# Turning node features with VectorE's 32x32 transposes and a hop through DRAM, in a two-layer graph network

## The chip, the cores and the metric

The kernel runs on one core of one Trainium2 chip. The metric is device time in microseconds (us), the median of the runs. The core's engines work side by side, each on its own in-order stream of instructions: TensorE (PE in the profile; its weight loads are PEld), VectorE (DVE), ScalarE (ACT), GpSimd (POOL) and the queue engine SyncE (SP), which here only issues DMA transfers. They wait for one another through semaphores.

## What is computed

There are 16 independent batches of 1024 nodes with 128 features each. Layer 0 is an attention with a gate, layer 1 has four heads with a tanh in place of a softmax, and each layer ends with a residual sum and a layer norm. Cut to what matters:

```python
# B, N, D, H = 16, 1024, 128, 4
def layer0(x, adj):
    h = x @ Ww.T + Wb
    e = (h @ A) @ h.T
    e = e + e.T
    scores = where(adj > 0, e, 0.0)
    attention = softmax(scores, axis=1) * adj
    hp = relu(attention @ h)
    ic = sigmoid(hp @ wi_u + x @ wi_x)         # fc, oc alike
    return oc * tanh(ic * hp + fc * x)

def layer1(X, adj):
    h = X @ conv_w[head] + conv_b[head]        # for each of 4 heads
    scores = h @ attn_w[head] @ h.T
    hh = relu(tanh(adj * scores) @ h)
    return relu(relu(mean_over_heads(hh)) + X)

x = layernorm(x + layer0(x, adj))
x = layernorm(x + layer1(x, adj))
```

Everything is float32. A layer norm needs the nodes on the partitions (a row of features along the free dimension), while the products of layer 1 need the features on the partitions. So each batch has two turns of a 1024 x 128 matrix: the result x1 of the first layer norm becomes x1T, and the sum over the heads, which stands as features x nodes, becomes rows again before the last layer norm.

## The kernel before

`P` and `D` are 128, `NB` is 8 (blocks of 128 nodes), `NH` is 2 (halves of 512 columns), `BH` is 4. Numbers as L385 in the profile are lines of the whole kernel. The pools, and the late weights, which are issued behind batch 0's loads on the sync queue:

```python
    consts = ctx.enter_context(tc.tile_pool(name="consts", bufs=1))
    adjp = ctx.enter_context(tc.tile_pool(name="adjp", bufs=2 * NB + 1))
    sb = ctx.enter_context(tc.tile_pool(name="sb", bufs=2))
    ps_sc = ctx.enter_context(tc.tile_pool(name="ps_sc", bufs=4, space=PSUM))
    ps_acc = ctx.enter_context(tc.tile_pool(name="ps_acc", bufs=1, space=PSUM))
# ...
    def load_late_weights():
        nc.sync.dma_start(cw_in[0:1], conv_b.rearrange("(o h) d -> o h d", o=1))
        nc.sync.dma_start(cw_in[1:P], conv_w[:, 0 : D - 1, :].rearrange("h f d -> f h d"))
        nc.sync.dma_start(cw_last, conv_w[:, D - 1 : D, :].rearrange("h f d -> f h d"))
        nc.sync.dma_start(aw, attn_w.rearrange("h i j -> i h j"))
```

Layer 0 is a generator: each `yield` is a point at which the caller goes on with something else. Its scores, softmax and products (some lines cut):

```python
    def layer0(b):
        xTb = sb.tile([P, N], F32, tag="xT", name=f"xT_{b}")
        nc.sync.dma_start(xTb, xT[b])
        adj_t[b] = []
        for j in range(NB):
            t = adjp.tile([P, N], F32, tag="adj", name=f"adj_{b}_{j}")
            nc.sync.dma_start(t, adjT[b, ts(j, P), :])
            adj_t[b].append(t)
        xb = sb.tile([P, NB, D], F32, tag="x", name=f"x_{b}", bufs=1)
        nc.sync.dma_start(xb, x[b].rearrange("(k p) d -> p k d", p=P))
        if b == 0:
            load_late_weights()
    # ... project_T -> qT, yield; project rows -> h, yield
        def score(j):
            raw[j] = sb.tile([P, N - j * P], F32, tag=f"raw{j}", name=f"raw_{b}_{j}", bufs=1)
            scored[j] = []
            for q in range(NH):
                # ... blocks known by symmetry are turned from raw (L261); a product gives
                # the others (L266), which ScalarE evicts to raw (L269)

        def front(j):
            s = sb.tile([P, N], F32, tag="s0", name=f"s0_{b}_{j}", bufs=3)
            for at0, at1, e in scored.pop(j):
                if at0 < at1:
                    nc.vector.scalar_tensor_tensor(
                        s[:, at0:at1], adj_t[b][j][:, at0:at1], 0.0, e,
                        op0=ALU.is_gt, op1=ALU.mult,
                    )
            nmax = sb.tile([P, 1], F32, tag="nmax", name=f"nmax_{b}_{j}", bufs=4)
            nc.vector.tensor_reduce(nmax, s, AX.X, ALU.max, negate=True)
            z = sb.tile([P, 1], F32, tag="z", name=f"z_{b}_{j}", bufs=4)
            nc.scalar.activation(s, s, AF.Exp, bias=nmax, accum_out=z)
            if b:
                nc.gpsimd.tensor_mul(s, s, adj_t[b][j])
            held[j] = s, z

        def middle(j):
            s, z = held[j]
            if not b:
                nc.vector.tensor_mul(s, s, adj_t[b][j])
            rz = sb.tile([P, 1], F32, tag="rz", name=f"rz_{b}_{j}", bufs=4)
            nc.vector.reciprocal(rz, z)
            hz = sb.tile([P, D], F32, tag="hz", name=f"hz_{b}_{j}", bufs=4)
            nc.scalar.mul(hz, h[:, j, :D], rz)
            held[j] = s, hz

        def back(j):
            s, hz = held.pop(j)
            for q in range(NH):
                nc.tensor.matmul(
                    acc[:, ts(q, 512)], hz, s[:, ts(q, 512)],
                    start=(j == 0), stop=(j == NB - 1),
                )

        ahead = 0 if b else 1
        for j in range(ahead + 1):
            score(j)
        front(0)
        yield
        for j in range(NB):
            if j + 1 < NB:
                if j + 1 + ahead < NB:
                    score(j + 1 + ahead)
                front(j + 1)
                yield
            middle(j)
            if j:
                back(j - 1)
            yield
        back(NB - 1)
    # ... hp rows, gate, tanh (L331 to L370)
        x1 = sb.tile([P, NB, D + 1], F32, tag="x1", name=f"x1_{b}")
        nc.gpsimd.memset(x1[:, :, 0:1], 1.0)
        yield from layernorm(u, x1[:, :, 1 : D + 1], f"0_{b}")
        x1_t[b] = x1
```

`BETWEEN` drives it: layer 0 of batch b + 1 advances one `yield` after each of the first 24 of the 32 steps of layer 1 of batch b. The turn of x1, one step of layer 1 and the end of layer 1:

```python
    def turn_x1(b):
        x1T = sb.tile([P, N], F32, tag="x1T", name=f"x1T_{b}")
        for q in range(NH):
            pt = small(f"pt1_{b}_{q}")
            for i in range(BH):
                nc.tensor.transpose(pt[:, ts(i, P)], x1_t[b][:, q * BH + i, 0:D], ident)
            nc.scalar.copy(x1T[:, ts(q, 512)], pt)
        x1T_t[b] = x1T

    def layer1_step(b, hd, m):
        x1T, h1, uT = x1T_t[b], h1_t[b, m], u_t[b, hd]
        adj = adj_t[b][m]
        # ... acc: the PSUM tile of this head
        s = sb.tile([P, N], F32, tag="s1", name=f"s1_{b}_{hd}_{m}", bufs=4)
        for q in range(NH):
            ps = ps_sc.tile([P, 512], F32, tag="sc", name=f"sc1_{b}_{hd}_{m}_{q}")
            nc.tensor.matmul(ps, x1T[:, ts(m, P)], uT[:, ts(q, 512)], start=True, stop=True)
            nc.vector.tensor_mul(s[:, ts(q, 512)], ps, adj[:, ts(q, 512)])
        nc.scalar.activation(s, s, AF.Tanh)
        def back():
            for q in range(NH):
                nc.tensor.matmul(
                    acc[:, ts(q, 512)], h1[:, ts(hd, D)], s[:, ts(q, 512)],
                    start=(m == 0), stop=(m == NB - 1),
                )
            # at m == NB - 1: the relu of acc is added to sum_t[b] (L431, L433)
        push(back)

    def layer1_end(b):
        x1 = x1_t[b][:, :, 1 : D + 1]
        y = sb.tile([P, NB, D], F32, tag="u", name=f"y_{b}", bufs=1)
        for q in range(NH):
            pt = small(f"pt2_{b}_{q}")
            for i in range(BH):
                nc.tensor.transpose(pt[:, ts(i, P)], sum_t[b][:, ts(q * BH + i, P)], ident)
            rows = slice(q * BH, (q + 1) * BH)
            nc.vector.scalar_tensor_tensor(
                y[:, rows, :], pt.rearrange("p (k d) -> p k d", d=D), 1.0 / H, x1[:, rows, :],
                op0=ALU.mult, op1=ALU.add,
            )
        nc.vector.scalar_tensor_tensor(y, y, 0.0, x1, op0=ALU.max, op1=ALU.add)
        yield
        yield from layernorm(y, y, f"1_{b}")
        nc.gpsimd.dma_start(out[b].rearrange("(k p) d -> p k d", p=P), y)
```

The order of everything:

```python
    first, join = layer0(0), None
    for step, _ in enumerate(first):
        if step == 2 * NB:
            join = join_weights()
        if step >= 2 * NB:
            next(join, None)
    for _ in join:
        pass
    turn_x1(0)

    BETWEEN = range(24)
    ENDING = (DELAY, DELAY + 2, DELAY + 4)
    end = None
    for b in range(B):
        nxt = layer0(b + 1) if b + 1 < B else None
        for hd in range(H):
            for m in range(NB):
                layer1_step(b, hd, m)
                if end is not None and hd == 0 and m in ENDING:
                    next(end, None)
                if nxt is not None and hd * NB + m in BETWEEN:
                    next(nxt, None)
                last = hd == H - 1
                # ... see the diff
        end = layer1_end(b)
    while pending:
        pending.popleft()()
    for _ in end:
        pass
```

`push` holds a step's second product back for `DELAY` = 2 steps, so that ScalarE has its tanh ready.

Of the kernel before, what the change touches and what calls it, by code (L numbers as in the profile page):

```python
# [21 lines left out]
def two_layer_adjacency_kernel(  # L22
# [28 lines left out]
    adjp = ctx.enter_context(tc.tile_pool(name="adjp", bufs=2 * NB + 1))  # L51
    sb = ctx.enter_context(tc.tile_pool(name="sb", bufs=2))
    ps_sc = ctx.enter_context(tc.tile_pool(name="ps_sc", bufs=4, space=PSUM))
    ps_acc = ctx.enter_context(tc.tile_pool(name="ps_acc", bufs=1, space=PSUM))
# [10 lines left out]

    a_in = consts.tile([P, P], F32, name="a_in")
    nc.sync.dma_start(a_in, A)
    ww_in = consts.tile([P, P], F32, name="ww_in")
    nc.sync.dma_start(ww_in, Ww)
# [12 lines left out]
    nc.gpsimd.memset(wb_row[:, D:G], 0.0)  # L82
    gate_u, gate_x = ident_g[:, D : D + 3], wwT_g[:, D : D + 3]

    for t, ws in ((gate_x, (wi_x, wf_x, wo_x)), (gate_u, (wi_u, wf_u, wo_u))):
        for g, w in enumerate(ws):
            nc.scalar.dma_start(t[:, g : g + 1], w.rearrange("(d o) -> d o", o=1))
        if t is gate_x:
            nc.scalar.dma_start(wb_row[:, :D], Wb.partition_broadcast(P))

    def load_late_weights():
        nc.sync.dma_start(cw_in[0:1], conv_b.rearrange("(o h) d -> o h d", o=1))
        nc.sync.dma_start(cw_in[1:P], conv_w[:, 0 : D - 1, :].rearrange("h f d -> f h d"))
        nc.sync.dma_start(cw_last, conv_w[:, D - 1 : D, :].rearrange("h f d -> f h d"))
        nc.sync.dma_start(aw, attn_w.rearrange("h i j -> i h j"))
# [118 lines left out]

    adj_t, x_t, x1_t = {}, {}, {}


    def layer0(b):
# [28 lines left out]
        held, raw, scored = {}, {}, {}  # L247

        def score(j):

            raw[j] = sb.tile([P, N - j * P], F32, tag=f"raw{j}", name=f"raw_{b}_{j}", bufs=1)
            scored[j] = []
            for q in range(NH):
                ps = ps_sc.tile([P, 512], F32, tag="sc", name=f"sc0_{b}_{j}_{q}")
                turned = min(max(j - q * BH, 0), BH)
                for i in range(turned):
                    k = q * BH + i  # L260
                    nc.tensor.transpose(ps[:, ts(i, P)], raw[k][:, ts(j - k, P)], ident)  # L261
                lo, at = q * 512 + turned * P, (q + 1) * 512
                scored[j].append((q * 512, lo, ps[:, : turned * P]))
                if lo < at:
                    new = raw[j][:, lo - j * P : at - j * P]
                    nc.tensor.matmul(  # L266
                        ps[:, turned * P :], qT[:, ts(j, P)], xTb[:, lo:at], start=True, stop=True
                    )
                    nc.scalar.activation(  # L269
                        new, ps[:, turned * P :], AF.Identity, bias=h[:, j, G - 1 : G]  # L270
                    )
                    scored[j].append((lo, at, new))

        def front(j):

            s = sb.tile([P, N], F32, tag="s0", name=f"s0_{b}_{j}", bufs=3)
            for at0, at1, e in scored.pop(j):
                if at0 < at1:
                    nc.vector.scalar_tensor_tensor(  # L279
                        s[:, at0:at1], adj_t[b][j][:, at0:at1], 0.0, e,  # L280
                        op0=ALU.is_gt, op1=ALU.mult,
                    )
            nmax = sb.tile([P, 1], F32, tag="nmax", name=f"nmax_{b}_{j}", bufs=4)
            nc.vector.tensor_reduce(nmax, s, AX.X, ALU.max, negate=True)  # L284
            z = sb.tile([P, 1], F32, tag="z", name=f"z_{b}_{j}", bufs=4)
            nc.scalar.activation(s, s, AF.Exp, bias=nmax, accum_out=z)  # L286
            if b:
                nc.gpsimd.tensor_mul(s, s, adj_t[b][j])  # L288
            held[j] = s, z

        def middle(j):

            s, z = held[j]
            if not b:
                nc.vector.tensor_mul(s, s, adj_t[b][j])
# [84 lines left out]
    def turn_x1(b):  # L380
        x1T = sb.tile([P, N], F32, tag="x1T", name=f"x1T_{b}")
# [89 lines left out]
    ENDING = (DELAY, DELAY + 2, DELAY + 4)  # L471
    end = None
    for b in range(B):
        nxt = layer0(b + 1) if b + 1 < B else None
        for hd in range(H):
            for m in range(NB):
# [8 lines left out]
                if last:  # L485
                    if m == NB - 4:
# [8 lines left out]
                elif m == NB - 3:  # L495
# [45 lines left out]
```

## Time and profile before

| what | value |
|---|---|
| time, median of 3 runs | 2555.05 us (2553.41 to 2555.42) |
| span of the profiled execution | 2551.7 us |
| GpSimd busy | 384.0 us, 15% of the span |
| DMA | 94.29 MB, mean 37 GB/s |
| products `sc` and `acc` of layer 1 on TensorE (L415, L421) | 963.9 and 962.0 us busy |
| products that turn x1 (L385) | 128, busy 17.7 us in sum |
| products that turn the head sums (L443) | 128, busy 16.8 us in sum |
| additions that take the turned sums from PSUM (L446) | 32 of 128x512, 686 ns each |
| copies of x1T out of PSUM on ScalarE (L386) | 32 of 128x512, 588 ns each |

How to read it: busy time is given for each engine and for each group of instructions, as a sum and as the mean of one. A group's line names the engine, the operation, the tile written, the tiles read and the shape. Idle time stands with what ended it. TensorE's instructions overlap one another, so the distance from one start to the next tells more of what it can do than the length of one. Every float32 product is listed as two instructions, a float32 transpose as one. DMA times run from the issue to the landing.

### The profile page before, as it was taken

The numbers are of one execution on the slowest core, as the hardware profiler recorded it, in microseconds if no ns is written. First come the engines' busy times: TensorE is split into PE (matmuls) and PEld (weight loads), VectorE is DVE, ScalarE is ACT, GpSimd is POOL, SyncE is SP. The second block draws the span as 40 slices with busy tenths as digits, with TensorE's granted clock in tenths as the row PEclk, the third lists the DMA queues.
The fourth block names the chain that finished last, engine by engine and source line by source line (L and its number), as shares of the span: only waits on it lengthen the run. The fifth ranks groups of instructions, "written<-read, shape, count | busy, mean of one in ns | idle before, by whom it ended". The sixth has DMA issues, their size and how long they took to land.

```text
span 2551.7 us, 20009 instructions
## 1 busy us (share of the span) xinstructions
PE 2504.9 (98%) x6818; PEld 1183.2 (46%) x6818; DVE 1423.7 (56%) x2977; ACT 1084.5 (43%) x1541; POOL 384.0 (15%) x211
## 2 busy tenths in 40 slices
PE   6999999999999999999999999999999999999997
PEld 3444444444444444444444444444444444444443
DVE  6555646555475554755456565564655646555454
ACT  4444444444443444444444344443444444444432
POOL 0110202102021110211202011020210202112000
PEclk9999999999999999999999999999999999999999
DMA  5002020020200102011020110202002020010000
GB/s 181 12 1 83 8 83 9 4 79 8 83 9 25 58 9 83 9 42 50 1 83 9 50 42 1 83 9 74 17 1 83 9 83 9 16 51 9 1 9 9
DMA packets 42269, 94.29 MB, mean 37 GB/s; under 512 B 3894, under 2 KB 21686, under 8 KB 42167
## 3 DMA queue, kind: packets, MB, share of 16 engines
q1 hardware_dynamic: 38855, 84.55, 10.5%
q0 software_dynamic: 2304, 8.39, 1.1%
q8 instruction: 54, 0.88, 0.2%
q14 instruction: 48, 0.39, 0.1%
q10 hardware_dynamic: 1008, 0.07, 0.0%
HBM read 84.61 MB, written 8.39 MB: 36 GB/s over the span
## 4 chain that ended last, share of the span: by engine, by line
PE 87%; DVE 7%; ACT 2%; issue 1%; SPq 1%; DMA 1%; POOL 0%; ACTq 0%; POOLq 0%
PE sc L415 32%; PE acc L421 32%; PE acc L305 8%; PE pR L394 4%; PE pT_u L197 3%; PE sc L266 2%; DVE s L279 2%; PE sc L261 2%; DVE nmax L284 1%; DVE s L416 1%; ACT s L417 1%; PE pt L340 1%; PE pR_h L239 1%; PE pT_q L197 1%; DVE st L180 1%
## 5 line engine op out<-in xcount | busy, mean ns | idle before, releaser
L416 DVE TENSOR_TENSOR s<-sc,adj 128x512 f32<-128x512 f32 x1024 | 683.4, 686 | 787.3 <-PE sc L415 772.3
L415 PE MATMUL sc<-uT,x1T 128*128 128x512 f32 x2048 | 963.9, 593 | 8.1 <-DVE s L279 8.1
L421 PE MATMUL acc<-s,h 128*128 128x512 f32 x2048 | 962.0, 592 | 0.0
L417 ACT ACTIVATE s<-s 128x1024 f32<-128x1024 f32 x512 | 541.5, 1058 | 834.1 <-DVE s L416 830.8
L421 PEld LDWEIGHTS acc<-s,h 128*128 128x128 f32 x2048 | 387.6, 190 | 491.3 <-issue 490.5
L415 PEld LDWEIGHTS sc<-uT,x1T 128*128 128x128 f32 x2048 | 382.1, 190 | 463.3 <-issue 391.5
L288 POOL TENSOR_TENSOR s<-s,adj 128x1024 f32<-128x1024 f32 x120 | 283.1, 2359 | 1494.8 <-PE sc L266 782.7
L286 ACT ACTIVATE s<-s,nmax 128x1024 f32<-128x1024 f32 x128 | 147.0, 1149 | 274.2 <-DVE nmax L284 272.1
L305 PE MATMUL acc<-s,hz 128*128 128x512 f32 x512 | 241.3, 593 | 5.9 <-ACT hz L299 5.9
L279 DVE SCALAR_TENSOR_TENSOR s<-adj,sc 128x512 f32<-128x512 f32 (+3 forms) x160 | 83.9, 526 | 157.5 <-ACT raw L269 89.2
L284 DVE TENSOR_REDUCE nmax<-s 128x1 f32<-128x1024 f32 x128 | 156.2, 1220 | 4.4
L305 PEld LDWEIGHTS acc<-s,hz 128*128 128x128 f32 x512 | 96.6, 190 | 129.0 <-issue 118.6
L269 ACT ACTIVATE raw<-sc,h 128x512 f32<-128x512 f32 (+1 forms) x192 | 107.2, 575 | 91.9 <-PE sc L266 90.4
L266 PE MATMUL sc<-xT,qT 128*128 128x512 f32 (+3 forms) x384 | 145.1, 487 | 0.0
L197 PE MATMUL pT_u<-x1T,ms 128*128 128x512 f32 x256 | 123.2, 604 | 0.1
L279 DVE SCALAR_TENSOR_TENSOR s<-adj,raw 128x512 f32<-128x512 f32 (+1 forms) x192 | 111.0, 598 | 7.3 <-ACT raw L269 4.7
L394 PE MATMUL pR<-cw,x1T 128*128 128x512 f32 x256 | 114.9, 592 | 0.0
L185 POOL TENSOR_TENSOR rs<-rs,mhalf 128x8 f32<-128x8 f32 x32 | 52.8, 1651 | 288.8 <-DVE rs L184 166.9
L397 ACT COPY h<-pR 128x512 f32<-128x512 f32 x128 | 74.9, 585 | 48.8 <-PE pR L394 48.8
L433 DVE SCALAR_TENSOR_TENSOR sum<-acc,sum 128x512 f32<-128x512 f32 x96 | 61.9, 686 | 46.4 <-PE acc L421 46.4
L352 POOL TENSOR_TENSOR u<-x,gate 128x1024 f32<-128x1024 f32 x16 | 30.5, 1907 | 342.5 <-DVE gate L350 342.5
L299 ACT ACTIVATE hz<-h,rz 128x128 f32<-128x128 f32 x128 | 50.4, 394 | 74.5 <-DVE rz L297 74.5
(89 smaller groups left out, 1126.7 us busy)
## 6 DMA issues: line engine op xcount, KB each, us to landing
adj<-in_adjT_dram SPq DMA_DIRECT2D x128, 512.0 KB, 3.7
xT<-in_xT_dram SPq DMA_DIRECT2D x16, 512.0 KB, 5.8
x<-in_x_dram SPq DMA_DIRECT2D x16, 512.0 KB, 5.1
out_dram<-y POOLq DMA_DIRECT2D x16, 512.0 KB, 3.9
aw<-in_L_gnn_attn_w_dram SPq DMA_DIRECT2D x1, 256.0 KB, 4.3
cw_in<-in_L_gnn_conv_w_dram SPq DMA_DIRECT2D x1, 254.0 KB
a_in<-in_L_gnn_A_dram SPq DMA_DIRECT2D x1, 64.0 KB, 2.3
ww_in<-in_L_gnn_Ww_dram SPq DMA_DIRECT2D x1, 64.0 KB, 2.4
```

The source lines that it names most:

```text
L197: nc.tensor.matmul(ps, w, src[:, ts(q, 512)], start=True, stop=True)
L266: nc.tensor.matmul(ps[:, turned * P :], qT[:, ts(j, P)], xTb[:, lo:at], start=True, stop=True)
L279: nc.vector.scalar_tensor_tensor(s[:, at0:at1], adj_t[b][j][:, at0:at1], 0.0, e, op0=ALU.is_gt, op1=ALU.mult,)
L284: nc.vector.tensor_reduce(nmax, s, AX.X, ALU.max, negate=True)
L286: nc.scalar.activation(s, s, AF.Exp, bias=nmax, accum_out=z)
L288: nc.gpsimd.tensor_mul(s, s, adj_t[b][j])
L305: nc.tensor.matmul(acc[:, ts(q, 512)], hz, s[:, ts(q, 512)], start=(j == 0), stop=(j == NB - 1),)
L394: nc.tensor.matmul(ps, x1T_t[b][:, ts(k, P)], cw.rearrange("p h d -> p (h d)"), start=True, stop=True)
L415: nc.tensor.matmul(ps, x1T[:, ts(m, P)], uT[:, ts(q, 512)], start=True, stop=True)
L416: nc.vector.tensor_mul(s[:, ts(q, 512)], ps, adj[:, ts(q, 512)])
L417: nc.scalar.activation(s, s, AF.Tanh)
L421: nc.tensor.matmul(acc[:, ts(q, 512)], h1[:, ts(hd, D)], s[:, ts(q, 512)], start=(m == 0), stop=(m == NB - 1),)
```

## The change

The kernel after turns x1 (batches 1 to 15) and the head sums (batches 0 to 14) without TensorE. VectorE transposes each 32x32 block of the tile in place of the whole, the result is written to a scratch tensor in DRAM, and four reads bring the blocks back to where a whole transpose would have put them. It is meant to take work from TensorE and copies from ScalarE, at the price of a way through DRAM that lasts longer; so the turn of x1 moves from step 4 of the last head to step 0, and the end of layer 1 waits three steps between its turn and its addition. Batch 0's x1 and batch 15's sums, beside which nothing else could run, keep the identity products.

Together with this goes another schedule for batch 0, whose layer 0 has nothing to run beside. The scores are no longer computed one block ahead, the multiplication by the adjacency goes to GpSimd as in the other batches, the late weights are loaded on GpSimd's queue rather than behind the loads of batch 0, x is loaded behind the first adjacency tile, and the joining of the layer 1 weights starts at step 5 instead of at step 16. The adjacency pool has one tile less. The projection for the next head comes at step 4 instead of step 5.

The diff, without blank lines and with one cut:

```diff
--- before.py
+++ after.py
@@ -48,9 +48,10 @@
     BH = NB // NH
     consts = ctx.enter_context(tc.tile_pool(name="consts", bufs=1))
-    adjp = ctx.enter_context(tc.tile_pool(name="adjp", bufs=2 * NB + 1))
+    adjp = ctx.enter_context(tc.tile_pool(name="adjp", bufs=2 * NB))
     sb = ctx.enter_context(tc.tile_pool(name="sb", bufs=2))
     ps_sc = ctx.enter_context(tc.tile_pool(name="ps_sc", bufs=4, space=PSUM))
+    dram = ctx.enter_context(tc.tile_pool(name="dram", bufs=2, space=bass.MemoryType.DRAM))
     ps_acc = ctx.enter_context(tc.tile_pool(name="ps_acc", bufs=1, space=PSUM))
     ctx.enter_context(tc.manual_schedule())
@@ loads of Ww and A change places; wb_row goes from the scalar to the sync queue: cut @@
 def load_late_weights():
-        nc.sync.dma_start(cw_in[0:1], conv_b.rearrange("(o h) d -> o h d", o=1))
-        nc.sync.dma_start(cw_in[1:P], conv_w[:, 0 : D - 1, :].rearrange("h f d -> f h d"))
-        nc.sync.dma_start(cw_last, conv_w[:, D - 1 : D, :].rearrange("h f d -> f h d"))
-        nc.sync.dma_start(aw, attn_w.rearrange("h i j -> i h j"))
+        nc.gpsimd.dma_start(cw_in[0:1], conv_b.rearrange("(o h) d -> o h d", o=1))
+        nc.gpsimd.dma_start(cw_in[1:P], conv_w[:, 0 : D - 1, :].rearrange("h f d -> f h d"))
+        nc.gpsimd.dma_start(cw_last, conv_w[:, D - 1 : D, :].rearrange("h f d -> f h d"))
+        nc.gpsimd.dma_start(aw, attn_w.rearrange("h i j -> i h j"))
@@ -212,6 +212,21 @@
                 bias_row.unsqueeze(1).to_broadcast([P, BH, D]),
             )
+    Q = 32
+    def turn(dst, src, name):
+        t = sb.tile([P, N], F32, tag="turn", name=f"turn_{name}", bufs=1)
+        nc.vector.transpose(t.rearrange("p (k d) -> p k d", d=P), src)
+        d = dram.tile([P, N], F32, tag="turn", name=f"dram_{name}")
+        nc.sync.dma_start(d, t)
+        dv = d.rearrange("(a i) (k c j) -> c i k a j", i=Q, c=P // Q, j=Q)
+        for c in range(P // Q):
+            nc.sync.dma_start(
+                dst[ts(c, Q)].rearrange("i (k a j) -> i k a j", a=P // Q, j=Q), dv[c]
+            )
     adj_t, x_t, x1_t = {}, {}, {}
@@ -224,10 +239,11 @@
             t = adjp.tile([P, N], F32, tag="adj", name=f"adj_{b}_{j}")
             nc.sync.dma_start(t, adjT[b, ts(j, P), :])
             adj_t[b].append(t)
-        xb = sb.tile([P, NB, D], F32, tag="x", name=f"x_{b}", bufs=1)
-        nc.sync.dma_start(xb, x[b].rearrange("(k p) d -> p k d", p=P))
-        if b == 0:
-            load_late_weights()
+            if j == 0:
+                xb = sb.tile([P, NB, D], F32, tag="x", name=f"x_{b}", bufs=1)
+                nc.sync.dma_start(xb, x[b].rearrange("(k p) d -> p k d", p=P))
+                if b == 0:
+                    load_late_weights()
         qT = sb.tile([P, N], F32, tag="qT0", name=f"qT0_{b}", bufs=1)
         h = sb.tile([P, NB, G], F32, tag="h0", name=f"h0_{b}", bufs=1)
@@ -244,15 +260,15 @@
         yield
         acc = ps_acc.tile([P, N], F32, tag="acc0", name=f"acc0_{b}")
-        held, raw, scored = {}, {}, {}
-        def score(j):
+        held, raw = {}, {}
+        def front(j):
             raw[j] = sb.tile([P, N - j * P], F32, tag=f"raw{j}", name=f"raw_{b}_{j}", bufs=1)
-            scored[j] = []
+            s = sb.tile([P, N], F32, tag="s0", name=f"s0_{b}_{j}", bufs=3)
             for q in range(NH):
                 ps = ps_sc.tile([P, 512], F32, tag="sc", name=f"sc0_{b}_{j}_{q}")
                 turned = min(max(j - q * BH, 0), BH)
@@ -260,7 +276,7 @@
                     k = q * BH + i
                     nc.tensor.transpose(ps[:, ts(i, P)], raw[k][:, ts(j - k, P)], ident)
                 lo, at = q * 512 + turned * P, (q + 1) * 512
-                scored[j].append((q * 512, lo, ps[:, : turned * P]))
+                parts = [(q * 512, lo, ps[:, : turned * P])]
                 if lo < at:
                     new = raw[j][:, lo - j * P : at - j * P]
                     nc.tensor.matmul(
@@ -269,30 +285,23 @@
                     nc.scalar.activation(
                         new, ps[:, turned * P :], AF.Identity, bias=h[:, j, G - 1 : G]
                     )
-                    scored[j].append((lo, at, new))
-        def front(j):
-            s = sb.tile([P, N], F32, tag="s0", name=f"s0_{b}_{j}", bufs=3)
-            for at0, at1, e in scored.pop(j):
-                if at0 < at1:
-                    nc.vector.scalar_tensor_tensor(
-                        s[:, at0:at1], adj_t[b][j][:, at0:at1], 0.0, e,
-                        op0=ALU.is_gt, op1=ALU.mult,
-                    )
+                    parts.append((lo, at, new))
+                for at0, at1, e in parts:
+                    if at0 < at1:
+                        nc.vector.scalar_tensor_tensor(
+                            s[:, at0:at1], adj_t[b][j][:, at0:at1], 0.0, e,
+                            op0=ALU.is_gt, op1=ALU.mult,
+                        )
             nmax = sb.tile([P, 1], F32, tag="nmax", name=f"nmax_{b}_{j}", bufs=4)
             nc.vector.tensor_reduce(nmax, s, AX.X, ALU.max, negate=True)
             z = sb.tile([P, 1], F32, tag="z", name=f"z_{b}_{j}", bufs=4)
             nc.scalar.activation(s, s, AF.Exp, bias=nmax, accum_out=z)
-            if b:
-                nc.gpsimd.tensor_mul(s, s, adj_t[b][j])
+            nc.gpsimd.tensor_mul(s, s, adj_t[b][j])
             held[j] = s, z
         def middle(j):
             s, z = held[j]
-            if not b:
-                nc.vector.tensor_mul(s, s, adj_t[b][j])
             rz = sb.tile([P, 1], F32, tag="rz", name=f"rz_{b}_{j}", bufs=4)
             nc.vector.reciprocal(rz, z)
             hz = sb.tile([P, D], F32, tag="hz", name=f"hz_{b}_{j}", bufs=4)
@@ -309,15 +318,10 @@
-        ahead = 0 if b else 1
-        for j in range(ahead + 1):
-            score(j)
         front(0)
         yield
         for j in range(NB):
             if j + 1 < NB:
-                if j + 1 + ahead < NB:
-                    score(j + 1 + ahead)
                 front(j + 1)
                 yield
             middle(j)
@@ -378,6 +382,10 @@
     x1T_t, h1_t, u_t = {}, {}, {}
     def turn_x1(b):
+        if b:
+            x1T_t[b] = sb.tile([P, N], F32, tag="x1T", name=f"x1T_{b}")
+            turn(x1T_t[b], x1_t[b][:, :, 0:D], f"x1_{b}")
+            return
         x1T = sb.tile([P, N], F32, tag="x1T", name=f"x1T_{b}")
         for q in range(NH):
             pt = small(f"pt1_{b}_{q}")
@@ -437,7 +445,11 @@
     def layer1_end(b):
         x1 = x1_t[b][:, :, 1 : D + 1]
         y = sb.tile([P, NB, D], F32, tag="u", name=f"y_{b}", bufs=1)
-        for q in range(NH):
+        if b + 1 < B:
+            turn(y.rearrange("p k d -> p (k d)"), sum_t[b].rearrange("p (k d) -> p k d", d=P), f"sum_{b}")
+            yield
+            nc.vector.scalar_tensor_tensor(y, y, 1.0 / H, x1, op0=ALU.mult, op1=ALU.add)
+        for q in range(NH if b + 1 == B else 0):
             pt = small(f"pt2_{b}_{q}")
             for i in range(BH):
                 nc.tensor.transpose(pt[:, ts(i, P)], sum_t[b][:, ts(q * BH + i, P)], ident)
@@ -455,9 +467,9 @@
     first, join = layer0(0), None
     for step, _ in enumerate(first):
-        if step == 2 * NB:
+        if step == 3:
             join = join_weights()
-        if step >= 2 * NB:
+        elif step > 3 and step % 2:
             next(join, None)
     for _ in join:
         pass
@@ -468,7 +480,7 @@
     BETWEEN = range(24)
-    ENDING = (DELAY, DELAY + 2, DELAY + 4)
+    ENDING = (DELAY, DELAY + 3, DELAY + 4, DELAY + 5)
     end = None
     for b in range(B):
         nxt = layer0(b + 1) if b + 1 < B else None
@@ -483,7 +495,7 @@
                 if last and b + 1 == B:
                     continue
                 if last:
-                    if m == NB - 4:
+                    if m == 0:
                         assert b + 1 in x1_t
                         turn_x1(b + 1)
                     elif m == NB - 3:
@@ -492,7 +504,7 @@
                         rows(b + 1, range(NB // 2))
                     elif m == NB - 1:
                         rows(b + 1, range(NB // 2, NB))
-                elif m == NB - 3:
+                elif m == NB - 4:
                     head_uT(b, hd + 1)
         end = layer1_end(b)
     while pending:
```

More of the change, by code (lines that the diff above doesn't have):

```diff
@@ L64, in two_layer_adjacency_kernel @@
     nc.gpsimd.memset(mhalf, -0.5)
+    ww_in = consts.tile([P, P], F32, name="ww_in")
+    nc.sync.dma_start(ww_in, Ww)
     a_in = consts.tile([P, P], F32, name="a_in")
     nc.sync.dma_start(a_in, A)
-    ww_in = consts.tile([P, P], F32, name="ww_in")
-    nc.sync.dma_start(ww_in, Ww)
     wb_col = consts.tile([P, 1], F32, name="wb_col")
@@ L82, in two_layer_adjacency_kernel @@
     nc.gpsimd.memset(wb_row[:, D:G], 0.0)
+    nc.sync.dma_start(wb_row[:, :D], Wb.partition_broadcast(P))
     gate_u, gate_x = ident_g[:, D : D + 3], wwT_g[:, D : D + 3]
@@ L87, in two_layer_adjacency_kernel @@
             nc.scalar.dma_start(t[:, g : g + 1], w.rearrange("(d o) -> d o", o=1))
-        if t is gate_x:
-            nc.scalar.dma_start(wb_row[:, :D], Wb.partition_broadcast(P))
     def load_late_weights():
-        nc.sync.dma_start(cw_in[0:1], conv_b.rearrange("(o h) d -> o h d", o=1))
-        nc.sync.dma_start(cw_in[1:P], conv_w[:, 0 : D - 1, :].rearrange("h f d -> f h d"))
-        nc.sync.dma_start(cw_last, conv_w[:, D - 1 : D, :].rearrange("h f d -> f h d"))
-        nc.sync.dma_start(aw, attn_w.rearrange("h i j -> i h j"))
+        nc.gpsimd.dma_start(cw_in[0:1], conv_b.rearrange("(o h) d -> o h d", o=1))
+        nc.gpsimd.dma_start(cw_in[1:P], conv_w[:, 0 : D - 1, :].rearrange("h f d -> f h d"))
+        nc.gpsimd.dma_start(cw_last, conv_w[:, D - 1 : D, :].rearrange("h f d -> f h d"))
+        nc.gpsimd.dma_start(aw, attn_w.rearrange("h i j -> i h j"))
     cw_in = sb.tile([P, H, D], F32, tag="s1", name="cw_in", bufs=4)
```

## The prediction, made before the change was run

> **What bounds the kernel now.** I read three things in turn: the page's busy shares, the list of what TensorE (PE) waited for, and the timelines of single engines around one batch boundary. The first line of the page's part 1 is busy time, share of the span, and instructions of each engine:
>
> ```profile
> PE 2504.9 (98%) x6818; PEld 1183.2 (46%) x6818; DVE 1423.7 (56%) x2977; ACT 1084.5 (43%) x1541; POOL 384.0 (15%) x211
> ```
>
> PE is idle for 46.8 us of 2551.7. Who made it wait (total us, times, longest):
>
> ```profile
> PE pt L385 <- DVE x L188: 12.4, 1, 12.4
> PE sc L415 <- DVE s L279: 8.1, 14, 0.6
> PE acc L305 <- ACT hz L299: 5.9, 7, 1.7
> ```
>
> The first and third are batch 0, whose layer 0 has nothing to overlap with; only the second belongs to the steady state, 0.58 us per batch. Most of the rest lies at the two ends of the run. So from batch 1 on PE has no holes, and every microsecond of PE work that disappears is a microsecond off the end, as long as no other engine makes PE wait. What the identity products cost PE is read from its timeline (start us, length us), at the turn of x1 and at the turn of the head sums:
>
> ```profile
> 207.41 1.04 PE L385 MATMUL pt<-ident,x 128*128 128x128 f32 x8
> 208.28 1.88 PE L415 MATMUL sc<-uT,x1T 128*128 128x512 f32 x4
> ...
> 240.99 1.04 PE L443 MATMUL pt<-ident,sum 128*128 128x128 f32 x8
> 241.86 1.88 PE L266 MATMUL sc<-xT,qT 128*128 128x512 f32 x4
> ```
>
> Start to start, eight products occupy PE for 0.87 us, 109 ns each, not the 273 ns that one is listed with.
>
> **What the skill says.** (1) The Trainium skill, "TensorE: Matmul & The Clock Gate", Part 4: PE-mode transpose, gives about 275 ns for a 128x128 transpose in a kernel. The trace has 273 ns as a duration, but these overlap; what can be saved is the 109 ns spacing. (2) "VectorE: DVE Perf Modes", The three transpose paths: VectorE transposes 32x32 blocks only, and the page warns that a DMA which transposes by strides is slow. The trace has no VectorE transpose; the change keeps 32 floats together, so its DMA moves runs of 128 bytes. (3) "DMA: Bandwidth & Descriptors", Anatomy of one DMA, puts some 2 us of fixed cost on each transfer. The trace agrees: the smallest loads, 0.5 KB, land after 2.4 us. (4) Same page, Why a DMA increments its semaphore by 16 and not by 1: a transfer uses the largest number of engines up to 16 that divides the slowest dimension on both sides, so 127 partitions get one engine. The trace agrees: after the load of 127 rows of conv weights the sync queue (SP) is stuck on its next issue for 14.19 us. The new reads have 32 partitions and so should use all 16.
>
> **The change, part by part.**
>
> *PE.* x1 is turned off PE for batches 1 to 15 and the sums for batches 0 to 14: 30 groups of eight, 30 x 0.87 = **26.1 us** less. All of it is on the bounding engine.
>
> *VectorE.* Each turn adds one 128x1024 transpose. I take 1.22 us, what the other one-pass 128x1024 operations here take (max-reduce 1.22, the add-relu 1.23): 30 x 1.22 = 36.6 us. The sums' two additions from PSUM (2 x 0.687) become one of about 1.22 us. VectorE goes from 1424 to about 1458 us, 58% of the span: not a bound. ScalarE loses 30 copies of 0.587 us, 17.6 us, which were beside other work. The end of layer 1 is now spread over steps 2, 5, 6 and 7 of the next batch's head 0 instead of 2, 4 and 6. I walked through the score buffers in PSUM: the 0.58 us wait comes while the row statistics (2.6 us) stand ahead of the masking. In the new order the score buffers come free in time, so I credit about half of it, **-4 us**.
>
> *The hop.* From the end of the transpose: one write to DRAM, a wait for it, four reads. The page's DMA part gives whole-tile transfers, and the DMA view of the first 12 us the small loads (packets, MB, share of 16 engines):
>
> ```profile
> out_dram<-y POOLq DMA_DIRECT2D x16, 512.0 KB, 3.9
> x<-in_x_dram SPq DMA_DIRECT2D x16, 512.0 KB, 5.1
> ```
> ```profile
> q10 hardware_dynamic: 1008, 0.07, 5.7%
> ```
>
> 5.7% of 16 x 12 us is 10.9 us for 1008 packets, about 11 ns each; nearly all of them carry 4 bytes. The one-engine weight load moved 508 runs of 512 bytes in about 14.2 us, 28 ns each. I interpolate 128 bytes at some 15 ns. A turn reads 4096 such runs, 256 per engine: 3.8 us. Write 3.9, semaphore 0.1, four issues at about 0.45 us each with the last starting 1.4 us after the first, then 2.4 us for a small transfer and the 64 runs of the last read (1 us): about **9 us**. Were a short run to cost as much as a 512-byte one, the reads take 7.2 us and the turn about 13.5.
>
> How long may it take? For x1, the timeline of VectorE at head 3, step 0:
>
> ```profile
> 192.14 2.14 DVE L188 TENSOR_SCALAR x<-u,mv,rs 128x128 f32<-128x128 f32 x8 [0.57 <-POOL rs L185]
> 194.20 2.48 DVE L416 TENSOR_TENSOR s<-sc,adj 128x512 f32<-128x512 f32 x4
> ```
>
> Normalization ends at 194.2, the masking of step 0 takes half of the next line, so the transpose runs from 195.5 to 196.7. The projection that reads x1T stays at step 5, where PE arrives at 211.72 - 0.87 = 210.85. Budget **14.2 us**, against 9. For the sums the transpose ends near 241.4 (masking of step 2 ends 240.2) and the addition comes behind the masking of step 5, which ended at 257.7 and would end near 255 without the 2.6 us of statistics. Budget about 13.7 us, and PE feels it only when VectorE is some 4 us late, for PSUM holds two steps. Both should be hidden. In the last batch there is no layer 0 beside it, so three steps are 3 x 3.44 = 10.3 us: a wait of perhaps **+1.5 us**, once.
>
> *Loads.* The adjacency pool shrinks from 17 to 16 tiles, so a load waits one step more. Layer 0 reads the tiles in batch order over 16 steps, starting two steps into head 0, and the loads take 3.7 us; this costs nothing. The hop stands in the same in-order SP queue, but the loads of the next batch cannot start before head 3 frees their buffers.
>
> *Batch 0.* Here the change undoes a schedule: no score is computed ahead, and the 128x1024 mask multiply goes from VectorE to GpSimd (1.22 against 2.36 us). Before, VectorE bounds this stage, 3.7 us per row block:
>
> ```profile
> 37.40 1.22 DVE L284 TENSOR_REDUCE nmax<-s 128x1 f32<-128x1024 f32 x1
> 38.54 1.22 DVE L295 TENSOR_TENSOR s<-s,adj 128x1024 f32<-128x1024 f32 x1
> ```
>
> After, the loop is a chain VectorE-ScalarE-VectorE: exp 1.2, row scaling 0.31, eviction of the new scores, their masking, max 1.22. With the listed durations row blocks 2 to 7 come every 4.6 down to 3.4 us, and three weight copies of 0.58 us are dropped into it. I get the last mask multiply on GpSimd ending at 49.7 and the last product there ending at 51.6 us, instead of 48.2. The joining of weights has left the tail, -1 us. Late weights on GpSimd's queue no longer block SP, but nobody waited for what was blocked. Net **+2.5 us**.
>
> Sum: 2555.05 - 26.1 - 4 + 1.5 + 2.5 = 2529; 3 us on top for small waits that I did not find: **2532 us**, 0.9% less.
>
> **Rivals.** *A. The turn arrives late for PE.* Four reads of short runs might cost over 30 ns a run, or the read may wait longer for the write to DRAM. For it: the budgets are only 5 us above my estimate, and no 128-byte transfer is in the trace. Against: the 11 ns of the 4-byte packets. At 41 ns a run the turn takes about 17 us; x1 is then some 3 us late, 15 times, 45 us, eating more than the gain: about 2575. At 60 ns both turns stall: over 2650. *B. VectorE becomes a local bound.* In head 0 the last steps of layer 1 now fall on three consecutive steps beside layer 0. For it: normalization of y takes 4.28 us there, beside GpSimd. Against: a pair of steps gives VectorE 5.4 us of 10.2. If PE lost 1 us per batch, 2550. *C. Batch 0 costs far more,* because the weights from GpSimd's queue arrive after step 5 and PE, in order, waits: up to 10 us, about 2540. *D. PE's waits vanish fully and batch 0 loses nothing:* 2523.
>
> **Range and chances.** The PE part is sure to 1 us; batch 0 to about 4; the steady waits to about 6; the heavy tail is rival A, to which I give 15%. Range 2520 to 2558. Over 2% faster would need 51 us, twice what PE can lose: 2%. Over 2% slower needs A at its harder end: 8%. Within 2%: 90%.
>
> **What would show it.** PE busy about 26 us less, with 240 fewer products; lines for VectorE transposes near 1.2 us; turn reads landing 9 us after the transpose; no PE wait on a DMA at the projection of x1T, none of VectorE at the sums' addition except in the last batch; first x1T product at about 66.5 instead of 64.2 us. A wait of PE for x1T, or of VectorE for y, in every batch would prove me wrong.

## The result and the profile after

The kernel after takes 2543.9 us (median of 4 runs, 2543.17 to 2544.18) against 2555.12 us before: ratio 0.9957, interval 0.994 to 0.9974. It is faster by 11 us (0.4%) where 23 were predicted, and it lies inside the predicted range of 2520 to 2558. The 11 us are the difference of two large numbers, as the profile shows. Its first line, then what TensorE (PE) waited for (total us, times, longest):

```profile
PE 2479.7 (98%) x6578; PEld 1162.7 (46%) x6578; DVE 1426.8 (56%) x2984; ACT 1080.3 (42%) x1511; POOL 409.3 (16%) x223
```
```profile
PE p_last L143 <- DMA cw_last<-in_L_gnn_conv_w_dram: 13.6, 1, 13.6
PE pt L393 <- DVE x L188: 12.3, 1, 12.3
PE acc L314 <- ACT hz L308: 7.0, 3, 3.2
...
PE acc L429 <- DVE sum L441: 2.6, 15, 0.2
```

PE is busy 25.2 us less, with 240 instructions fewer, as it should be. Three things are new in the list: a wait of 13.6 us on a transfer of weights, in batch 0; a wait of 0.17 us for the addition to the head sums, once per batch; and the absence of the 14 waits for VectorE's masking. PE's timeline in batch 0 (start, length, in brackets the idle time ahead and what ended it) shows the first, and where batch 0 ends:

```profile
21.38 1.46 PE L282 MATMUL sc<-xT,qT 128*128 128x256 f32 x4
36.40 2.04 PE L143 MATMUL p_last<-cw_last,but_first 1*128 1x512 f32 x2 [13.56 <-DMA cw_last<-in_L_gnn_conv_w_dram]
...
70.50 5.37 PE L314 MATMUL acc<-s,hz 128*128 128x512 f32 x8 [3.21 <-ACT hz L308]
76.55 2.05 PE L344 MATMUL pt<-ident_g,hpT 128*128 128x131 f32 x16 [0.69 <-ACT hpT L335]
```
```profile
90.95 2.18 PE L393 MATMUL pt<-ident,x 128*128 128x128 f32 x8 [12.34 <-DVE x L188]
```

The same turn in the kernel before:

```profile
64.24 2.19 PE L385 MATMUL pt<-ident,x 128*128 128x128 f32 x8 [12.38 <-DVE x L188]
```

The first turn of x1 starts at 90.95 us instead of 64.24: batch 0 lost 26.7 us. From there to the end of the span the kernel after needs 2542.4 - 90.95 = 2451.5 us and the kernel before 2551.7 - 64.24 = 2487.5: the steady part gained 36.0 us. Both halves differ from the prediction, in opposite directions.

The hop is there as planned. VectorE's transposes, the sync queue around one turn of x1, and the transfers of the page (median us from issue to landing):

```profile
L221 DVE STREAM_TRANSPOSE turn_x<-x x15: 1232/1235/1240, 221.8 to 2376.1; 128x1024 f32<-128x1024 f32 x15
```
```profile
223.07 0.33 SPq L223 DMA_DIRECT2D dram_x<-turn_x  x1
225.66 3.37 SPq L226 DMA_DIRECT2D x1T<-dram_x  x4
229.13 0.69 SPq L236 DMA_DIRECT2D xT<-in_xT_dram  x1
```
```profile
dram_x<-turn_x SPq DMA_DIRECT2D x15, 512.0 KB, 2.6
x1T<-dram_x SPq DMA_DIRECT2D x60, 128.0 KB, 3.4
```

The write takes 2.6 us, the four reads are issued in 3.4 us and each lands some 3.4 us after its issue. PE comes to the projection that needs x1T at 237.65, about 14.6 us behind the end of the transpose, and does not wait.

### The profile page after: what moved, and what is told of

It reads as the page before. It is cut to its first block, busy times and chain, and to the rows that moved or that the text cites. A ratio compares the mean times of both kernels' runs of the same rounds, so it can differ in the third digit from the quotient of the medians.

```text
span 2542.4 us, 19811 instructions
## 1 busy us (share of the span) xinstructions
PE 2479.7 (98%) x6578; PEld 1162.7 (46%) x6578; DVE 1426.8 (56%) x2984; ACT 1080.3 (42%) x1511; POOL 409.3 (16%) x223
## 3 DMA queue, kind: packets, MB, share of 16 engines
q1 hardware_dynamic: 167072, 115.56, 15.1%
## 4 chain that ended last, share of the span: by engine, by line
PE 91%; DVE 5%; POOL 1%; DMA 1%; issue 1%; ACT 0%; POOLq 0%
PE acc L429 33%; PE sc L423 31%; PE acc L314 9%; PE sc L282 5%; PE pT_u L197 4%; PE pR L402 4%; PE sc L277 2%; DVE s L424 1%; DVE x L188 1%; DMA cw_last<-in_L_gnn_conv_w_dram 1%; PE pt L344 1%; POOL rs L185 1%; PE pR_h L255 1%; PE pT_q L197 1%; DVE turn_x L221 1%
## 5 line engine op out<-in xcount | busy, mean ns | idle before, releaser
L299 POOL TENSOR_TENSOR s<-s,adj 128x1024 f32<-128x1024 f32 x128 | 302.0, 2360 | 1497.2 <-ACT s L298 1497.2
L291 DVE SCALAR_TENSOR_TENSOR s<-adj,raw 128x512 f32<-128x512 f32 (+1 forms) x192 | 119.3, 634 | 34.9 <-ACT raw L285 32.9
L199 ACT COPY uT<-pT_u 128x512 f32<-128x512 f32 x128 | 73.2, 583 | 39.2 <-PE pT_u L197 39.0
L277 PEld LDWEIGHTS sc<-ident,raw 128*128 128x128 f32 x448 | 55.8, 142 | 58.5 <-issue 51.2
```

The costliest lines, as they stand in the source:

```text
L291: nc.vector.scalar_tensor_tensor(s[:, at0:at1], adj_t[b][j][:, at0:at1], 0.0, e, op0=ALU.is_gt, op1=ALU.mult,)
```

## The experiments

Eleven kernels were run, in three groups, each group with its own runs of the kernel before (medians 2554.42, 2554.22 and 2554.61 us). The outcome first:

| run | batch 0 | steady part | us | ratio to before, interval |
|---|---|---|---|---|
| e1 | before | after | 2518.56 | 0.9859, 0.9843 to 0.9876 |
| e2 | after | before | 2580.47 | 1.0101, 1.0086 to 1.0116 |
| e3 | after, weights joined late | after | 2534.98 | 0.9925, 0.991 to 0.994 |
| e4 | after, weight rows split | after | 2533.62 | 0.992, 0.9905 to 0.9935 |
| e5 | e3, mask multiply on VectorE | after | 2525.3 | 0.9889, 0.9874 to 0.9904 |
| e6 | e5, scores one block ahead | after | 2519.73 | 0.9866, 0.9851 to 0.9881 |
| e7 | before | only x1 turned on VectorE | 2547.68 | 0.9974, 0.9965 to 0.9984 |
| e8 | before | before, projection one step earlier | 2537.82 | 0.9937, 0.9922 to 0.9951 |
| e9 | before | after, x1 turned at step 1 | 2512.85 | 0.9836, 0.9821 to 0.9851 |
| e10 | before | after, x1 turned at step 3 | 2543.04 | 0.9957, 0.9944 to 0.9969 |
| e11 | before | only the sums turned on VectorE | 2525.15 | 0.9886, 0.9871 to 0.9901 |

### Taking the two halves apart: e1 and e2

The edit of e1 puts batch 0 back and keeps everything later:

```diff
 # kernel before, with turn(), its use for x1 and the sums, 16 adjacency tiles, and
-    ENDING = (DELAY, DELAY + 2, DELAY + 4)
+    ENDING = (DELAY, DELAY + 3, DELAY + 4, DELAY + 5)
-                    if m == NB - 4:          # turn_x1(b + 1)
+                    if m == 0:
-                elif m == NB - 3:            # head_uT(b, hd + 1)
+                elif m == NB - 4:
```

e2 is the reverse: the kernel after without `turn()` and with these three lines as before.

> Batch 0 as in the kernel before, everything after it as in the kernel after (turns on VectorE with the hop, end of layer 1 at steps 2, 5, 6, 7, next projection at step 4, 16 adjacency tiles). In the two traces the first turn of x1 starts at 90.9 us instead of 64.2, so batch 0 lost 26.7 us and all the rest gained about 36 to 38. Theory (the two parts are independent): 2544 - 26.7 = 2517 us, first turn near 64 us. Rival (the turns bring only the 26.1 us of products, and the rest of the gain belongs to the new schedule of batch 0): 2529 us or more.

> The kernel before with nothing but the new schedule of batch 0 (late weights on GpSimd's queue, joining from step 5, no score ahead, mask multiply on GpSimd, order of the first loads, 16 adjacency tiles). Theory: the schedule alone costs 26.7 us, so 2582 us with the first turn of x1 near 91 us. Rival (batch 0 is late because the hops stand in the sync queue): about 2555 us.

Measured: 2518.56 and 2580.47 us. The halves add up to within about 1 us: -36 and +26 make -10, against -11 for the whole change. In e2 the long wait is there without any hop (PE's waits):

```profile
PE p_last L142 <- DMA cw_last<-in_L_gnn_conv_w_dram: 14.0, 1, 14.0
```

So the new schedule of batch 0 cost 26 us, and beyond that 1 us neither half depends on the other. e1 alone beats both kernels.

### What batch 0 lost: e3, e4, e5, e6

```diff
 # e3: the kernel after, with
-        if step == 3:
+        if step == 2 * NB:
             join = join_weights()
-        elif step > 3 and step % 2:
+        if step >= 2 * NB:
             next(join, None)
```

> The kernel after, with the weights joined from step 16 as before, still loaded on GpSimd's queue. Theory (TensorE stands in order behind the product that needs cw_last, which lands at 36 us): the 13.6 us wait goes, and with it some 4 us that TensorE loses at half clock behind it, while about 1 us comes back at the end of layer 0: 2527 us, no wait on a transfer in batch 0. Rival (the chain of scores, masking, exponential and the multiply on GpSimd sets the pace anyway, and the wait only hides in it): 2540 us.

```diff
 # e4: the kernel after, with
-        nc.gpsimd.dma_start(cw_in[1:P], conv_w[:, 0 : D - 1, :].rearrange("h f d -> f h d"))
+        for lo, hi in ((1, 113), (113, P)):
+            nc.gpsimd.dma_start(cw_in[lo:hi], conv_w[:, lo - 1 : hi - 1, :].rearrange("h f d -> f h d"))
```

> The kernel after, with the 127 rows of conv weights loaded as 112 and 15 rows on the same queue. Theory (127 rows go through a single DMA engine, and cw_last queues behind them there): the weights land by about 15 to 20 us, the wait of TensorE shrinks from 13.6 to below 2 us, 2529 us. Rival (the weights are late because they share the DMA engines with 5 MB of tiles): they still land at about 30 us and the time stays near 2543.

Measured: 2534.98 and 2533.62 us, 8.9 and 10.3 us less than the kernel after. The wait is gone in both, but I had expected 17 and 15: part of the wait's 13.6 us had hidden other waits that now show. In e3 PE's waits for `hz`, the scaled rows of `h`, grow from 7.0 to 15.3 us. In e4 the weights come early, but PE now waits 2.7 us for xT, and its first scores start at 16.88 us instead of 14.84. e4 tells why the weights were late. First the DMA view of the kernel after, first 40 us (issues, KB, us to landing), then that of e4:

```profile
cw_in<-in_L_gnn_conv_w_dram POOLq DMA_DIRECT2D x1, 254.0 KB, 33.4
...
cw_last<-in_L_gnn_conv_w_dram POOLq DMA_DIRECT2D x1, 2.0 KB, 29.0
```
```profile
cw_in<-in_L_gnn_conv_w_dram POOLq DMA_DIRECT2D x1, 224.0 KB, 8.3
...
cw_last<-in_L_gnn_conv_w_dram POOLq DMA_DIRECT2D x1, 2.0 KB, 8.7
```

127 rows in one transfer land after 33.4 us and hold the 2 KB behind them; as 112 and 15 rows they land after 8 to 9 us, beside the same 6.49 MB on the sync queue. The rival, crowding by the tiles, falls. It is rather the tiles that were held up: in the same two views the median adjacency tile lands after 14.1 us in the kernel after and after 10.1 in e4. While PE waited it also lost its clock, which stood at 0.50 from 28 to 44 us. Stretches of the kernel after (stretch, its length, then busy us of PE and of the others, granted clock, DMA share, GB/s):

```profile
24.00:28.00 4.00, 0.00 (x0) 0.00 (x0) 2.07 (x5) 2.47 (x5) 1.24 (x1) 0.87 1.03 317
28.00:32.00 4.00, 0.00 (x0) 0.00 (x0) 3.20 (x3) 0.73 (x1) 1.10 (x1) 0.50 0.14 50
32.00:36.00 4.00, 0.00 (x0) 0.00 (x0) 0.00 (x0) 0.52 (x2) 2.34 (x1) 0.50 0.06 23
...
40.00:44.00 4.00, 4.00 (x10) 2.10 (x9) 0.29 (x1) 0.37 (x1) 0.00 (x0) 0.50 0.00 0
```

In the third stretch the DMA share of 0.06 is one engine of 16 at work, and 23 GB/s fit that: the one-engine load of the kernel before moved 512 bytes in 28 ns, 18 GB/s.

With the wait gone, e3 still starts its first turn at 82.05 us, 17.8 later than before. GpSimd's multiply and VectorE's masking, from the timelines of e3:

```profile
38.43 2.35 POOL L299 TENSOR_TENSOR s<-s,adj 128x1024 f32<-128x1024 f32 x1 [3.42 <-ACT s L298]
```
```profile
39.25 2.08 DVE L291 SCALAR_TENSOR_TENSOR s<-adj,raw 128x512 f32<-128x512 f32 x1 [1.58 <-ACT raw L285]
41.36 1.22 DVE L296 TENSOR_REDUCE nmax<-s 128x1 f32<-128x1024 f32 x1
```

A masking of 128x512 lasts 2.08 us instead of 0.69, and it ends 0.55 us after GpSimd does. The narrower ones of the next row blocks, 384, 256 and 128 columns, end 0.40, 0.29 and 0.15 us after it, each about 0.14 us less than it lasts alone in e5 (0.55, 0.42, 0.28): they stand until the multiply is over. That made the next pair of runs:

```diff
 # e5: e3, with
-            nc.gpsimd.tensor_mul(s, s, adj_t[b][j])
+            if b:
+                nc.gpsimd.tensor_mul(s, s, adj_t[b][j])
 # and in middle(j)
+            if not b:
+                nc.vector.tensor_mul(s, s, adj_t[b][j])
```

> As e3 (kernel after, weights joined late), and in batch 0 the multiply by the adjacency back on VectorE. In e3 a masking of VectorE that reads two SBUF tiles takes 1.5 to 2.1 us whenever GpSimd multiplies, and ends 0.4 to 0.5 us behind it; alone it takes 0.28 to 0.69. Theory (GpSimd's multiply holds VectorE's masking, about 1.4 us in each of 7 row blocks): 2535 - 10 = 2525 us, maskings of 0.28 to 0.69 us, row blocks some 4 us apart instead of 5.4. Rival (the chain is slow because no score is computed ahead, so that eviction waits for the exponential): 2533 us, row blocks still over 5 us apart.

```diff
 # e6: e5, with score(j) and front(j) apart as in the kernel before, and
+        ahead = 0 if b else 1
+        for j in range(ahead + 1):
+            score(j)
```

> As e5, and in batch 0 each score computed one block ahead as before; only the first loads and the queue of the late weights are still those of the kernel after. Theory: row blocks 3.7 us apart, bound by VectorE as before, and what is left against e1 (2518.6) is the later start, 1.4 us: 2520 us. Rival (late weights on GpSimd's queue cost more than the start, by crowding the first tiles): 2525 us or more.

Measured: 2525.3 and 2519.73 us. In e5 the same masking is short again, and the row blocks come every 4.0 to 4.7 us instead of every 5.2 to 6.0 (the reduction of the next block starts at 40.78):

```profile
35.90 0.69 DVE L291 SCALAR_TENSOR_TENSOR s<-adj,raw 128x512 f32<-128x512 f32 x1 [0.46 <-ACT raw L285]
36.63 1.22 DVE L296 TENSOR_REDUCE nmax<-s 128x1 f32<-128x1024 f32 x1
37.77 1.22 DVE L307 TENSOR_TENSOR s<-s,adj 128x1024 f32<-128x1024 f32 x1
```

Summed over the seven row blocks, the maskings that read `raw` last 9.3 us longer in e3 than in e5, nearly all of what e5 gains; that GpSimd's multiply is itself longer (2.35 against 1.22 us) matters little. So of the 25.3 us between the kernel after and e1, undone in this order, 8.9 go to the wait for weights, 9.7 to GpSimd's multiply in the way of the masking, and 5.6 to the scores no longer ahead. The 1.2 us left for the order and queues of the first loads are no more than the scatter of the runs. The rival of e5 was not idle: the missing lead cost 5.6 us. But it is the smaller part.

### What the steady part gained: e7, e8, e9, e10, e11

```diff
 # e8: the kernel before, with
-                elif m == NB - 3:
+                elif m == NB - 4:
                     head_uT(b, hd + 1)
```

> The kernel before with one line changed: the next head's projection at step 4 instead of 5. Score buffers in PSUM go round by four; with the projection at step 5 the scores of step 6 need the two buffers of layer 0's third row block, which VectorE reads late. With it at step 4 they need those of step 5, free long before. Theory: the 0.58 us wait goes, 14 times: 2554.4 - 8.1 = 2546 us. Rival (the wait comes from where the row statistics stand, and goes only when the end of layer 1 is moved): 2554 us, wait still there.

Measured: 2537.82 us. The rival falls, the wait is gone; but the gain is 16.4 us, twice the 8.1 of the list of waits. PE's timelines around the place, kernel before and then e8, show why:

```profile
255.71 1.46 PE L266 MATMUL sc<-xT,qT 128*128 128x256 f32 x4
257.18 1.98 PE L197 MATMUL pT_u<-x1T,ms 128*128 128x512 f32 x4
259.75 1.98 PE L415 MATMUL sc<-uT,x1T 128*128 128x512 f32 x4 [0.58 <-DVE s L279]
261.57 1.88 PE L421 MATMUL acc<-s,h 128*128 128x512 f32 x4
```
```profile
252.31 1.88 PE L197 MATMUL pT_u<-x1T,ms 128*128 128x512 f32 x4
254.02 1.88 PE L415 MATMUL sc<-uT,x1T 128*128 128x512 f32 x4
255.74 1.88 PE L421 MATMUL acc<-s,h 128*128 128x512 f32 x4
```

Start to start, the projection and the scores behind it take 2.57 + 1.82 us in the first and 1.71 + 1.72 in the second, 0.96 us apart, and 0.18 more lies in the products ahead. The bracket of 0.58 counts only time in which no product was under way by the modelled ends. From the first product of step 3 to that of step 8 (243.58 to 269.85 against 243.82 to 268.98) e8 is 1.11 us shorter. In the 14 batches that have the wait this makes 15.5, and the spans of the two profiled executions differ by 15.3.

```diff
 # e7: e1, without the turn in layer1_end, ENDING and the projection as before
 # e11: e1, without the turn in turn_x1, which comes at m == NB - 4 again
```

> As e1, but the head sums are turned by identity products again, with the end of layer 1 at steps 2, 4, 6 and the next projection at step 5. Theory (each group of eight products is worth its 0.87 us of TensorE, and the 0.58 us wait per batch belongs to the order of the steps): 2554.4 - 13 = 2541 us, with the 8.1 us of waits for the masking still there. Rival (the hop through DRAM disturbs the steps near it and costs part of it): 2545 or more.

> As e1, but x1 is turned by identity products at step 4 of the last head again; only the head sums go through VectorE and DRAM. Theory (this turn costs nothing beside its 13 us of products saved): e8 (2537.8) - 13 = 2525 us, no wait of VectorE for the sums' addition. Rival (the addition at step 5 comes late and VectorE stands still for it): 2530 us or more.

Measured: 2547.68 us for e7, so the turn of x1 by itself gained 6.5 us instead of 13; its rival was right, something near it costs 6 us. And 2525.15 us for e11, 12.7 below e8: the turn of the sums gives all of its 13 and costs nothing. What e7 loses shows in PE's timeline of the kernel after (e7 has the same wait, 15 times):

```profile
223.51 1.88 PE L423 MATMUL sc<-uT,x1T 128*128 128x512 f32 x4
225.56 1.95 PE L429 MATMUL acc<-s,h 128*128 128x512 f32 x4 [0.16 <-DVE sum L441]
227.35 1.88 PE L423 MATMUL sc<-uT,x1T 128*128 128x512 f32 x4
```

2.05 + 1.79 us start to start instead of 1.72 + 1.72, 0.4 us in every batch. The last head's first accumulating product needs the accumulator, which VectorE has yet to add to the sums; and VectorE's transpose stands ahead of that addition. The next two runs move the transpose:

```diff
 # e9 and e10: e1, with
-                    if m == 0:
+                    if m == 1:               # e10: m == 3
                         assert b + 1 in x1_t
                         turn_x1(b + 1)
```

> As e1, but the turn of x1 stands at step 1 of the last head instead of step 0. In e1 and e7 the products of x1 save 13 us but the time falls by 6 to 7 less than that. In the traces the transpose (1.24 us) stands on VectorE ahead of the last addition to the head sums, and TensorE's first product of the next head waits for that addition, because there is one accumulator: 0.4 us start to start, in each batch. Theory: behind the addition the transpose holds up nobody, the hop of 8.6 us still ends before step 5: 2518.6 - 6.3 = 2512 us, that wait gone. Rival (VectorE's 1.24 us are missing in this stage wherever they stand, or the hop costs it): 2518 us.

> As e1, but the turn of x1 stands at step 3 of the last head. The transpose then ends near 230.8 us on the time scale of the kernel after's trace, and TensorE comes to the projection at about 237.3. Theory (the hop takes 8.6 us from the end of the transpose to the last landing): TensorE waits some 2.1 us at the projection in each of 15 batches: 2512 + 32 = 2544 us. Rivals: the hop takes 6 us or less: 2512, no wait; it takes the 13.5 us of the dear 128-byte runs: 2512 + 105 = 2617 us.

Measured: 2512.85 and 2543.04 us, where 2512 and 2544 were expected (e10 scatters, 2538.5 to 2552.6 in eight runs). In e9 the waits for the addition are no longer in the list, and it is the fastest kernel of this study: 1.6% below the kernel before. In e10 PE waits for the hop:

```profile
PE pT_u L198 <- DMA x1T<-dram_x: 25.6, 15, 2.5
```

In the batch whose transpose runs from 202.70 to 203.94, the projection starts at 212.09: the hop took at most 8.2 us there. In the trace of the kernel after, the last read lands 7.9 to 9.9 us behind the end of the transpose, over all 30 turns.

## Why the prediction came out as it did

**The products: right.** 26.1 us were expected from 240 products at 109 ns. e8 to e11 to e9 takes off 12.7 and then 12.3 us, 25.0 together.

**The hop: right, with offsetting terms.** 9 us were predicted; the kernel after shows 7.9 to 9.9. The write took 2.6 us instead of 3.9, the issues some 3.4 instead of 1.8. (The fixed cost of some 2 us, under (3) of the prediction, is stated by its page for transfers from GpSimd's queue; the 0.5 KB loads of 2.4 us set beside it were on ScalarE's queue.) The runs of 128 bytes are cheap: the sync queue's share of the DMA engines rose from 10.5% of 16 x 2551.7 us to 15.1% of 16 x 2542.4, some 1860 us; less 3840 writes of 4 KB at 195 ns, the mean of the output queue's packets before, this leaves about 9 ns for each of 122,880 reads, an estimate, where I had 15. Both budgets held (14.6 us against the 14.2 for x1), rival A did not come, and the last batch, for which I had added 1.5 us, did not wait.

**VectorE: half right.** The transpose takes 1.235 us (1.22 predicted) and VectorE is no bound. But the saving of x1's products came out whole only in e9. I asked what x1T's reader would wait for, not what the transpose itself would hold up: the addition behind it, and with it the one accumulator. That cost 0.4 us a batch, 5.7 us by e9 against e1.

**The steady wait: right that it goes, wrong size.** I credited -4 us, half of the list's 8.1. e8 shows 16.4, and one line of the change, the projection at step 4, suffices. I had put the wait down to the statistics in the way and its end to the later end of layer 1; e8 leaves both as they were, and what removes the wait is that the buffers asked for are free. No run moves the end of layer 1 alone. The term was mis-sized because I took the list of waits for the loss instead of measuring start to start, which I had done for the products a few lines earlier.

**Batch 0: wrong, and this is the step that failed.** Predicted +2.5 us, measured +26: the first turn of x1, expected at about 66.5 us, starts at 90.95. Three errors lie in it. First, "late weights on GpSimd's queue no longer block SP, but nobody waited for what was blocked": I knew that 127 rows go through one engine, and had the 14.19 us for it, but did not carry it over to the other queue nor ask when the weights land; PE stood 13.6 us. Rival C named this wait and sized it at 10 us, which is what e3 and e4 give back. Second, the chain was summed "with the listed durations"; masking beside GpSimd's multiply does not have them, 9.7 us. Third, the scores no longer ahead; my chain did count this, and it is most of the 3.4 us that I had for the loop against the 5.6 us measured.

The sum by the runs: -25.0 for the products, -16.4 for the projection, +5.7 for the transpose's place, +25.3 for batch 0, together -10.4, against -11.2 measured. The prediction named a time 12 us too low: 22.8 us too little for batch 0, 5.7 for the transpose's place and 1.1 for the products, against 12.4 us of gain too little for the steady wait and 4.5 for waits that did not come. In sum this is 12.7 us, of which 11.9 were measured. That the measured time still lies in the stated range is luck: it took two large errors of opposite sign.

## What to carry to other kernels

On an engine without holes, count what a stall costs from start to start of its instructions; the list of waits showed half of it here. When work moves to an idle engine, look for what stands behind it there in order, and for what it shares: a transpose ahead of an addition, and a multiply beside a masking, took back 6 and 10 us that no busy share showed. A load whose rows divide badly over the DMA engines was slow on both queues tried here, and the place to join it is behind its landing.

## What had not been expected of the hardware

Masking on VectorE with both inputs in SBUF stands still while GpSimd multiplies out of SBUF (2.08 us instead of 0.69, ending 0.55 us behind the multiply). The Trainium skill, "SBUF — State Buffer", Who interferes with whom, says that a VectorE instruction with two SBUF inputs contends with a GpSimd instruction that reads SBUF, and that one with at most one SBUF input, outside the modes that use both ports, does not. The runs agree on both: in e3 a masking with its scores in PSUM runs beside the multiply and keeps the 0.42 us that it has without it in e5.

```profile
27.44 0.42 DVE L291 SCALAR_TENSOR_TENSOR s<-adj,sc 128x256 f32<-128x256 f32 x1 [1.89 <-ACT raw L285]
```

The load of 127 rows from GpSimd's queue behaved like a one-engine transfer, 33.4 us against 8.3 for 112 rows. The page "DMA: Bandwidth & Descriptors", Why a DMA increments its semaphore by 16 and not by 1, allows that some direct copies from that queue spread 127 partitions over 16 engines; this one did not.

A VectorE transpose of 32x32 blocks over 128x1024 float32 takes 1.235 us, as much as the max-reduce (1.22) and the add-relu (1.23) of that size. A read of 4096 runs of 128 bytes, in four transfers, was there 5.5 us after its first issue (206.56 to 212.09 us in the batch of e10 above).
